# Anchoring row work behind pair work in the attention stripes of a four-layer graph network, and a new order of matmuls in its wide layer-2 pass

## The chip, the cores and the metric

The kernel runs on one core of a Trainium2 chip. The metric is the device time of one launch in microseconds (us). The kernel before was timed three times: 1152.08, 1147.19 and 1141.33 us, median 1147.19. One more execution was profiled: 1140.81 us, with a span of 1139.1 us from the first to the last instruction that the profile records, at a mean granted TensorE clock of 0.972. All single durations below come from that execution.

## The reference, cut to what matters

`x` has 4096 rows of 64 numbers; `adj` is a 4096 x 4096 matrix of zeros and ones. Four layers follow each other; each adds its result to its input and normalizes the rows. All four read the whole of `adj`.

```python
# layer 0: mean over neighbours, a linear layer, relu, rows to length 1
deg = clip(adj.sum(1) + 1, 1);  h = (adj @ X + X) / deg
out = relu(concat([X, h], 1) @ W + b);  out = out / max(norm(out), 1e-12)
# layers 1 and 3: attention in hyperbolic space
left, right = x_t @ w_att[:D], x_t @ w_att[D:]          # x_t = logmap0(x)
adj_att = sigmoid(left[:, None] + right[None, :] + b) * adj
x_local = logmap(x[:, None, :], x[None, :, :])          # a vector for each pair of rows
out = proj(expmap(x, einsum('ij,ijd->id', adj_att, x_local)))
# layer 2: halving weights by the rank of a neighbour, counted from the end of the row
support = x @ weight;  rank = cumsum(adj, 1)
k = min(deg, 100);  pos = rank - (deg - k)
out = (adj * where(pos > 0, 0.5 ** (k - pos), 0)) @ support + bias
# after every layer
x = layernorm(x + out)
```

## The kernel before, in words

**Tiling.** The 4096 target rows are four *groups* of 1024 (`GROUPS`, taken 3, 2, 1, 0), the 4096 source rows 32 *blocks* of 128 (`BLOCKS`, taken 31 to 0). A *stripe* is one group's pass over all source rows. Within a stripe the loop variable g runs from 15 to 0 and covers two blocks; `load(s, g)` on the SyncE queue (SP) brings their 1 MB of edges into one of six buffers, so all of `adj` (64 MB) is read once a layer. The text calls such a step of two blocks, inside a stripe, a *group of two blocks*, and numbers the eight attention stripes 0 to 3 (layer 1) and 4 to 7 (layer 3).

**Pair work in attention** (`attend`, L924 to L973). For each block six matmuls make z in PSUM for 128 x 1024 pairs (L945, L948, L951, two halves each); ScalarE (ACT) makes the sigmoid (L953) and a square of z (L956); VectorE (DVE) makes t1 (L959, per block) and, for both blocks at once, t2 (L961). PE then adds t2 into `acc` with four fp32 matmuls (L965, eight records in the trace). z, sig, sq and t have two buffers each. At the end of a stripe ACT copies `acc` to `sums` (L972).

**Row work.** What has to be done for a finished stripe's 1024 rows is written as Python generators. `later` puts one in one of two queues; after each block and each t2 `tick(rate)` runs the steps that are due, in both queues, until a step yields a wait (1 in the attention layers). rate is 1, but 2 in stripe 0 and 4 in stripe 4. Row PSUM buffers are two, taken by `take` after `free`. The generators that matter here:

- `move` (L982 to L1086) turns `sums` into the rows of the next layer's x: matmuls with `centre` (L1000), ACT's copy to u (L1002, twice), GpSimd's product w_att (L1007), the sums uu (L1011) and d (L1013) on DVE, then some 70 small DVE operations of 128 x 8 (k at L1015, three inverse square roots with the lines L673 to L679, tanh on ACT between, L1046 and on), at last GpSimd's w_att (L1081) and DVE's x (L1085).
- `linear` (L1088 to L1112) makes layer 2's products of those rows: transposes (L1095), ACT's copy x_t (L1100), matmuls (L1106), and `supports`, ACT's and DVE's `halves` (L1116, L1117).
- `spread_left` (L906 to L922) prepares the next group's left terms (L914 on PE); it is put in the second queue at g == 4 of the stripe before and is needed at the next stripe's start.
- `norm_rows` and `prepare` do the layer norm and the operands of the next attention layer.

After stripe n > 0 `attention` (L1280 to L1295) puts into the first queue `linear` (in layer 1) or `store` (in layer 3) of the group before, and then the move of the group just done. Only in the last stripe does `linear` go to the second queue, with a wait of 9.

**What sets the order.** In layers 0 and 2 a `manual_schedule` block keeps PE and ACT in the order of the source. In the attention layers (1 and 3) no such block holds: a scheduler places the instructions of every engine by what they depend on and by its own estimates, so a row step may end up ahead of pair work that stands before it in the source. Each engine then runs its list in order.

**Layer 2.** `wide_pass` (L1323 to L1351) takes groups 3 and 2 together: for each block and each of the two, `count` (L1386, four matmuls of 128 columns' weights) updates z, then the waiting `add_up` of the stripe-block before (L1401, four matmuls of 64-column weights) runs, then ACT makes the exponential (L1395). `narrow_pass` does groups 1 and 0 alone. `check` (L751) is a DVE operation over a loaded 128 x 2048 that sets a flag; every second load of layers 0 and 2 has one.

After layer 3 follow the last move, the last store and a few small checks: the *tail*. A second, general path of the kernel (behind a branch) isn't run here.

Of the kernel before, what the change touches and what calls it, by code (L numbers as in the profile page):

```python
# [19 lines left out]
P = 128  # L20
# [38 lines left out]
def gnn_stack_kernel(  # L59
# [509 lines left out]
    def stream(fits):  # L569

        with ExitStack() as st:
# [17 lines left out]
            FIXED = {mybir.EngineType.PE, mybir.EngineType.Activation}  # L589
            queues, place, done, held = ([], []), [0, 0], set(), []  # L590

            def tick(n):
                for _ in range(n):
                    place[1] += 1
                    for queue in queues:
                        while queue and queue[0][1] <= place[1]:
                            wait = next(queue[0][0], None)
                            if wait is None:
                                queue.pop(0)
                                continue  # L600
                            queue[0][1] = place[1] + wait
                            if wait:
                                break

# [3 lines left out]
            def in_turn(tag, *parts):  # L608
                for part in parts:
                    yield from (part or ())  # L610
                done.add(tag)

# [16 lines left out]
            def near():  # L629

                return 3 if place[0] == 0 else 1

# [36 lines left out]
            def rsqrt(a, name):  # L669
# [10 lines left out]
                return r  # L680

# [73 lines left out]
            def curved(c, name, least):  # L755


                c2, sc, rsc, of_y, root, short = (
                    num(keep, name + n, 1)
                    for n in ("_c2", "_sc", "_rsc", "_of_y", "_root", "_short")  # L760
# [3 lines left out]
                V.tensor_mul(root, rsc, c)  # L764
                V.tensor_scalar(of_y, rsc, -((2.0 * UNIT) ** -0.5), None, ALU.mult)
# [3 lines left out]
                return c, c2, sc, rsc, of_y, root, short  # L769
# [21 lines left out]
            def prepare(layer, s, att, b_att, curve, least, good, small):  # L791


                c, c2, sc, rsc, of_y, root, short = curve
# [187 lines left out]
            def move(layer, s, sums, curve):  # L982
# [3 lines left out]
                c, c2, sc, rsc, of_y, root, short = curve  # L986
# [22 lines left out]
                yield near()  # L1009
                yield soon()  # L1010
# [4 lines left out]
                V.scalar_tensor_tensor(k, d, c2, sum_1, ALU.mult, ALU.add)  # L1015
                V.tensor_mul(k, k, rb[:, at])

                kx, t2, xt = nums("kx"), nums("t2"), nums("xt")
                V.tensor_mul(kx, k, x2g)
                V.scalar_tensor_tensor(t2, d, -2.0, kx, ALU.mult, ALU.add)  # L1020
                V.tensor_mul(t2, t2, k)
                V.tensor_add(t2, t2, uu)
                V.tensor_scalar(t2, t2, 1e-30, None, ALU.max)
                V.tensor_sub(xt, d, kx)
                yield soon()
# [3 lines left out]
                V.scalar_tensor_tensor(un, t2, root, rsqrt(t2, "r_t2"), ALU.mult, ALU.mult)  # L1029
                V.tensor_scalar(un, un, fac, short, ALU.mult, ALU.max)  # L1030
                th = nums("th")
                V.reciprocal(r_un, un)
                yield after(29)
                nc.scalar.activation(th, un, AF.Tanh, scale=lam)
                yield near()
                V.scalar_tensor_tensor(un, r_un, fac, th, ALU.mult, ALU.mult)

                y2, xy, den, p, q = (nums(n) for n in ("y2", "xy", "den", "p", "q"))
                V.scalar_tensor_tensor(y2, un, c, un, ALU.mult, ALU.mult)
                V.scalar_tensor_tensor(xy, un, c2, xt, ALU.mult, ALU.mult)  # L1040
                V.tensor_mul(q, b[:, at], un)
                V.tensor_mul(y2, y2, t2)
                V.tensor_scalar(xy, xy, -1.0, 1.0, ALU.mult, ALU.add)
                V.tensor_mul(p, q, k)
                V.tensor_mul(den, cx2[:, at], y2)
                V.tensor_add(y2, xy, y2)  # L1046
                V.tensor_add(den, den, xy)
                V.tensor_sub(p, y2, p)
                V.tensor_scalar(den, den, 1e-15, None, ALU.max)
                V.reciprocal(den, den)  # L1050
                yield soon()
                V.tensor_mul(p, p, den)
                V.tensor_mul(q, q, den)

                px, qd, w2, t = nums("px"), nums("qd"), nums("w2"), nums("mt")
                V.tensor_mul(px, p, x2g)
                V.tensor_mul(qd, q, d)
                V.tensor_mul(t, q, q)
                V.scalar_tensor_tensor(w2, qd, 2.0, px, ALU.mult, ALU.add)
                V.tensor_mul(t, t, uu)  # L1060
                V.tensor_mul(w2, w2, p)
                V.tensor_add(px, px, qd)
                V.tensor_add(w2, w2, t)
                V.tensor_scalar(t, w2, least, None, ALU.max)
                yield soon()
                n = rsqrt(t, "n")
                V.tensor_scalar(n, n, rsc, 1.0, ALU.mult, ALU.min)
                yield soon()

                V.tensor_mul(w2, w2, n)  # L1070
                V.tensor_mul(p, p, n)
                V.tensor_mul(q, q, n)
                V.scalar_tensor_tensor(w2, px, 2.0, w2, ALU.mult, ALU.add)
                V.tensor_mul(w2, w2, n)
                V.tensor_add(w2, w2, x2g)
                V.tensor_scalar(w2, w2, 1.0 / D, 1e-5, ALU.mult, ALU.add)
                r = rsqrt(w2, "n")
                V.scalar_tensor_tensor(p, p, 1.0, r, ALU.add, ALU.mult)
                V.tensor_mul(q, q, r)  # L1079
                yield soon()  # L1080
                nc.gpsimd.tensor_mul(w, xg, over(p))  # L1081
                V.tensor_mul(u, u, over(q))
                yield soon()
                yield soon()
                V.tensor_add(x_of(layer + 1)[:, at, :], u, w)  # L1085
                yield after(72)  # L1086
# [193 lines left out]
            def attention(layer, curve, rates, behind):  # L1280

                need((layer, GROUPS[0]))
                for n, s in enumerate(GROUPS):
                    if n:
                        need((layer, s, "left"))
# [224 lines left out]
```

## Time and profile before

| What | us |
|---|---|
| Median of three runs | 1147.19 |
| Profiled execution | 1140.81 |
| Its span | 1139.1 |
| Layer 0 and stripe 0, to stripe 0's last t2 | 277.5 |
| Stripes 1, 2, 3 (from one last t2 to the next) | 81.2, 86.4, 87.2 |
| Layer 2's first exponential | at 529.2 |
| Layer 2's wide pass, two narrow passes | to 638.4, to 700.7, to 772.2 |
| Stripe 4's last t2 | at 863.9 |
| Stripes 5, 6, 7 | 81.2, 81.1, 83.4 |
| Tail, from stripe 7's last t2 to the end | 1109.6 to 1139.1 |

A row of the profile's timeline gives the start in us, the duration, engine, source line, operation, output and inputs with their shape, and in brackets how long the engine stood idle before it and which instruction released it. A row of the costliest groups gives the instructions' total busy time, the mean of one in ns, and the idle time ahead of them. A row of the waits gives which instruction waited for which, the total idle time, how often, and the longest.

### The profile page before, as it was taken

How to read it: one execution, taken by the hardware profiler on the slowest of the kernel's cores; microseconds unless marked ns; L12 is line 12 of the kernel's file. 1: busy time of each engine (PE TensorE's matmuls, PEld its weight loads, DVE VectorE, ACT ScalarE, POOL GpSimd, SP SyncE). 2: the span in 40 equal slices, each digit the busy share in tenths (PEclk: the TensorE clock that was granted, in tenths of full speed). 3: DMA queues.
4: the chain of work that ended last, by engine and by line, in shares of the span. 5: the costliest groups of instructions: out<-in, count | busy, mean ns of one | idle time of the engine just before them, and what ended most of it. 6: DMA issues, size and time to landing. Idle time of an engine off the chain costs nothing.

```text
span 1139.1 us, 13626 instructions
## 1 busy us (share of the span) xinstructions
PE 1021.6 (90%) x4949; PEld 391.2 (34%) x4949; DVE 956.0 (84%) x1882; ACT 821.2 (72%) x894; POOL 66.1 (6%) x97
## 2 busy tenths in 40 slices
PE   6999897899999899998999997798899999998981
PEld 3545544233333333332333232232333333333320
DVE  6687898999999899999653476528999999999996
ACT  0003216899989789787766778888898998987970
POOL 0020120000000000100100020000000001001001
PEclk8999998999999999999999999899999999999995
DMA  8999998545666466564988976676455665665500
GB/s 342 422 391 405 373 415 337 196 166 203 215 206 219 154 209 221 180 204 154 322 305 301 341 263 233 233 257 231 164 206 188 218 222 194 222 221 183 196 0 23
DMA packets 38419, 271.58 MB, mean 238 GB/s; under 512 B 4550, under 2 KB 4550, under 8 KB 5574
## 3 DMA queue, kind: packets, MB, share of 16 engines
q1 hardware_dynamic: 37440, 269.50, 65.8%
q10 hardware_dynamic: 902, 1.12, 0.3%
q8 instruction: 41, 0.67, 0.2%
q14 instruction: 36, 0.29, 0.1%
HBM read 269.55 MB, written 1.05 MB: 238 GB/s over the span
## 4 chain that ended last, share of the span: by engine, by line
DVE 53%; PE 29%; ACT 8%; DMA 6%; POOL 2%; issue 2%; ACTq 0%; SPq 0%; POOLq 0%; DVEq 0%
DVE t L959 21%; DVE t L961 20%; PE z L1386 10%; DMA edges<-in_adj_dram 6%; PE acc L1401 5%; PE acc L1243 4%; PE acc L965 2%; ACT sig L953 2%; ACT sq L956 2%; ACT sq L1395 1%; PE aux L1106 1%; PE aux L852 1%; PE z L945 1%; DVE junk L751 1%; PE z L951 1%
## 5 line engine op out<-in xcount | busy, mean ns | idle before, releaser
L953 ACT ACTIVATE sig<-left_b,right 128x1024 f32<-128x1024 f32 x256 | 293.8, 1149 | 46.5 <-DVE t L959 36.5
L959 DVE SCALAR_TENSOR_TENSOR t<-z,sig 128x1024 f32<-128x1024 f32 x256 | 310.0, 1216 | 5.9 <-ACT sq L956 5.0
L956 ACT ACTIVATE sq<-z,turn 128x1024 f32<-128x1024 f32 x256 | 281.5, 1106 | 22.8 <-PE z L951 20.7
L961 DVE SCALAR_TENSOR_TENSOR t<-sq,t 128x2048 f32<-128x2048 f32 x128 | 292.9, 2288 | 0.7
L965 PE MATMUL acc<-t,xe 128*64 128x512 f32 x1024 | 255.2, 611 | 28.5 <-DVE t L961 24.4
L945 PE MATMUL z<-edges,two_i 128*128 128x512 bf16 x512 | 201.7, 394 | 21.5 <-DVE t L959 21.5
L951 PE MATMUL z<-dst,src 74*128 74x512 f16 x512 | 195.2, 381 | 0.0
L948 PE MATMUL z<-lo_hi,hi_lo 128*128 128x512 f16 x512 | 194.1, 379 | 0.0
L1395 ACT ACTIVATE sq<-z,at_edge 128x512 bf16<-128x512 f32 (+1 forms) x192 | 153.0, 830 | 53.3 <-PE z L1386 51.9
L965 PEld LDWEIGHTS acc<-t,xe 128*64 128x64 f32 x1024 | 63.6, 137 | 163.0 <-DVE t L961 85.9
L751 DVE SCALAR_TENSOR_TENSOR t<-edges 128x2048 bf16<-128x2048 f32 x32 | 74.0, 2312 | 44.2 <-DMA edges<-in_adj_dram 44.1
L1386 PE MATMUL z<-edges,pass_by 128*128 128x512 bf16 x248 | 89.6, 401 | 15.9 <-ACT sq L1395 15.8
L945 PEld LDWEIGHTS <-two_i 128*128 128x128 bf16 x512 | 50.2, 98 | 143.8 <-issue 96.6
L1243 PE MATMUL acc<-edges,first 128*128 128x512 bf16 x256 | 80.6, 396 | 20.0 <-DMA edges<-in_adj_dram 19.8
L1386 PE MATMUL z<-edges,enter 128*128 128x512 bf16 x256 | 90.8, 397 | 0.0
L1401 PE MATMUL acc<-sq,halves 128*64 128x512 bf16 x512 | 82.6, 401 | 3.6 <-ACT sq L1395 2.9
L1243 PE MATMUL acc<-edges,third 128*65 128x512 bf16 x256 | 80.5, 396 | 0.0
L751 DVE SCALAR_TENSOR_TENSOR junk<-edges 128x2048 bf16<-128x2048 f32 x32 | 73.1, 2285 | 4.7 <-DMA edges<-in_adj_dram 4.5
L948 PEld LDWEIGHTS <-hi_lo 128*128 128x128 f16 x512 | 50.3, 98 | 68.8 <-issue 25.5
L951 PEld LDWEIGHTS <-src 74*128 74x128 f16 x512 | 49.2, 96 | 67.5 <-issue 2.3
L1081 POOL TENSOR_TENSOR w_att<-x,p 128x512 f32<-128x512 f32 x8 | 12.9, 1615 | 495.0 <-DVE q L1079 495.0
L1243 PEld LDWEIGHTS <-first 128*128 128x128 bf16 x256 | 24.1, 98 | 48.9 <-issue 21.3
(262 smaller groups left out, 771.3 us busy)
## 6 DMA issues: line engine op xcount, KB each, us to landing
edges<-in_adj_dram SPq DMA_DIRECT2D x256, 1024.0 KB, 4.9
x<-in_x_dram SPq DMA_DIRECT2D x4, 256.0 KB
out_dram<-x ACTq DMA_DIRECT2D x4, 256.0 KB
w_sb<-in_L_gnn_W_dram ACTq DMA_DIRECT2D x1, 32.0 KB, 5.1
given<-in_L_gnn_b_dram ACTq DMA_DIRECT2D x1, 0.2 KB
given<-in_L_gnn_bias_dram ACTq DMA_DIRECT2D x1, 0.2 KB
given<-in_L_gnn_b_att_dram ACTq DMA_DIRECT2D x1, 0.0 KB
given<-in_L_gnn_att_b_dram ACTq DMA_DIRECT2D x1, 0.0 KB
```

The source lines that it names most:

```text
L751: V.scalar_tensor_tensor(junk, a, 0.0, a, ALU.not_equal, ALU.not_equal, accum_out=odd[:, n : n + 1])
L945: nc.tensor.matmul(half, two_i, edge[:, at : at + W], start=True, stop=False)
L948: nc.tensor.matmul(half, hi_lo[:, of], lo_hi[:, to], start=False, stop=False)
L951: nc.tensor.matmul(half, src[:, of], dst[:, to], start=False, stop=True)
L953: nc.scalar.activation(sig, left_b, AF.Sigmoid, bias=right[:, j : j + 1])
L956: nc.scalar.activation(sq[:, k], zp, AF.Square, bias=turn, scale=-1.0 / UNIT)
L959: V.scalar_tensor_tensor(t[:, k], zp, 0.0, sig, ALU.max, ALU.mult)
L961: V.scalar_tensor_tensor(t, sq, HIGH**2, t, ALU.add, ALU.mult)
L965: nc.tensor.matmul(acc[h * D : (h + 1) * D, :], xe[:, j, :], t[:, k, h * W : (h + 1) * W], start=j == BLOCKS[0], stop=j == BLOCKS[-1],)
L1243: nc.tensor.matmul(accs[h][:m], lhs[:, j, :], edge[:, at : at + W], start=j == BLOCKS[0], stop=j == BLOCKS[-1],)
L1386: nc.tensor.matmul(z[:, h : h + W], lhs, rhs[:, h : h + W], start=j == BLOCKS[0], stop=True, skip_group_check=True,)
L1395: nc.scalar.activation(w, z[:, :n], AF.Exp, bias=at_edge, scale=-LN2)
```

## The change

- `mark` is called by `tick` ahead of the row steps and after them. It goes through the instructions written since its last call. Those on PE, ACT and DVE written outside the row steps are noted as the last pair instruction of their engine; each written by a row step gets a dependency without a semaphore, for the scheduler alone, on that last pair instruction. So in the scheduler's list it can't stand ahead of it. This holds in stripes with n > 0 (`anchored`), so not in stripes 0 and 4.
- `linear` and `store` of the group before go to the second queue in every stripe n > 0, with a wait of 9, and start only when the move of that group is through (`there`).
- In `wide_pass` both counts of a block come first, each with its exponential, and then both `add_up`s of the block before. Both accumulators are allocated at the start, and the two exponentials of a block share one buffer.
- In `move` the helper class `Small` is used with `on_pool` False, so all its operations stay on DVE. The reciprocal `r_un` of `un` is replaced by two operations on the inverse root (`by_root`, `by_short`, constants made once in `curved`), and one more yield stands behind d.

The instructions of PE, ACT, GpSimd and SP are the same in number; DVE gets 12 more small ones.

```diff
+            def mark(rows):
+                traced = nc.cur_bb.bb.instructions
+                for i in traced[seen[0] :]:
+                    if i.engine not in ROW_ENGINES:
+                        continue
+                    if not rows:
+                        pairs_last[i.engine] = i
+                    elif anchored[0] and i.engine in pairs_last:
+                        tc.add_manual_dep(
+                            i, pairs_last[i.engine].name,
+                            mybir.DependencyInfo(
+                                mybir.DependencyClass.NoSync, mybir.DependencyReason.DATA
+                            ),
+                            reason="row work behind the pairs",
+                        )
+                seen[0] = len(traced)
 
             def tick(n):
                 for _ in range(n):
                     place[1] += 1
+                    mark(False)
                     for queue in queues:
...
+                    mark(True)
...
+            def there(tag):
+                while tag not in done:
+                    yield 1
...
                 yield soon()
                 V.tensor_reduce(d, w, AX.X, ALU.add)
                 yield soon()
-                V.scalar_tensor_tensor(k, d, c2, sum_1, ALU.mult, ALU.add)
+                yield soon()
+                G.stt(k, d, c2, sum_1, ALU.mult, ALU.add)
...
-                V.reciprocal(r_un, un)
+                G.ts(r_un, r, by_root, 1.0 / fac, ALU.mult, ALU.mult)
+                G.ts(r_un, r_un, by_short, None, ALU.min)
...
+                    anchored[0] = n > 0
                     then = GROUPS[n + 1] if n + 1 < NW else None
                     sums = attend(layer, s, rates[n], then)
-                    move_s = move(layer, s, sums, curve)
+                    move_s = in_turn((layer, s, "moved"), move(layer, s, sums, curve))
                     if n:
-                        last = n + 1 == NW
-                        later(in_turn((layer + 1, s + 1), behind(s + 1)), last, 9 * last)
+                        later(
+                            in_turn((layer + 1, s + 1), there((layer, s + 1, "moved")), behind(s + 1)),
+                            True, 9,
+                        )
                     later(move_s)
                     if n + 1 == NW:
                         later(in_turn((layer + 1, s), behind(s)))
+                anchored[0] = False
...
-                accs = [None, None]
+                accs = [ps.tile([P, W], F32, name="acc") for _ in two]
...
+                        w = sb.tile([P, 2, WW], F32, name="sq").bitcast(BF16)[:, :, :WW]
                         for i, edge in enumerate(edges):
                             here = edge[:, k * WW : (k + 1) * WW]
                             count(zs[i], behind[i], here, j, WW)
                             behind[i] = here
-                            while lag:
-                                lag.pop(0)()
-                            w = weights_of(zs[i], WW)
-
-                            def add(i=i, j=j, w=w):
-                                if accs[i] is None:
-                                    accs[i] = ps.tile([P, W], F32, name="acc")
-                                add_up(accs[i], j, w[:, :W], w[:, W:])
-
-                            lag.append(add)
+                            weights_of(zs[i], WW, w[:, i])
+                            if i == 1:
+                                for of, acc in enumerate(accs if lag else ()):
+                                    add_up(acc, *lag[of])
+                                lag = [(j, w[:, n, :W], w[:, n, W:]) for n in range(2)]
```

## The prediction, made before the changed kernel ran

> **What bounds the kernel now.** I read the busy shares first, then the chain that ended last, then windows of each stage, then single groups of instructions.
>
> ```profile
> PE 1021.6 (90%) x4949; PEld 391.2 (34%) x4949; DVE 956.0 (84%) x1882; ACT 821.2 (72%) x894; POOL 66.1 (6%) x97
> DVE 53%; PE 29%; ACT 8%; DMA 6%; POOL 2%; issue 2%; ACTq 0%; SPq 0%; POOLq 0%; DVEq 0%
> 200.00:300.00 100.00, 91.27 (x429) 33.65 (x428) 95.74 (x134) 91.07 (x93) 3.47 (x8) 1.00 0.56 190
> 610.00:630.00 20.00, 20.00 (x105) 5.69 (x103) 4.83 (x6) 14.20 (x14) 0.00 (x0) 1.00 0.94 341
> ```
>
> The windows give sum, then PE, PEld, DVE, ACT and POOL busy, the granted clock, the DMA share and GB/s. In the attention stripes (200 to 300) PE, DVE and ACT are all nearly full; in the wide pass of layer 2 (610 to 630) PE never rests. An average can't tell which of three full engines sets a stripe, so I took one undisturbed group (two blocks) apart:
>
> ```profile
> 211.95 1.94 PE L965 MATMUL acc<-t,xe 128*64 128x512 f32 x8
> 213.02 0.15 DVE L679 SCALAR_TENSOR_TENSOR n_r<-rs_t,n_r 128x8 f32<-128x8 f32 x1
> 213.10 1.21 DVE L959 SCALAR_TENSOR_TENSOR t<-z,sig 128x1024 f32<-128x1024 f32 x1
> 213.82 0.40 PE L945 MATMUL z<-edges,two_i 128*128 128x512 bf16 x1
> 218.56 0.40 PE L945 MATMUL z<-edges,two_i 128*128 128x512 bf16 x1
> ```
>
> Groups start 4.74 us apart. PE's own work is 12 z matmuls at 0.2225 (2.67), 1.86 for the accumulation and about 0.2 for two changes between them: 4.73. DVE has t1 twice at 1.14 and t2 at 2.2, 4.47 in all, plus 0.085 for a small row operation slipped between (213.02 to the next start at 213.10). So three row operations in a group are free, and everything beyond is paid; every PE row matmul is paid at once (L1000 1.05 a call, layer 2's linear about 3.5 a group of rows). Both engines are the bound, group by group. DMA isn't: its share here is 0.56.
>
> **Anchoring the rows (`mark`) and the linear in the second queue.** Neither removes an instruction on PE or ACT, and DVE gains 12 (two scalings for one reciprocal in each of eight moves, and four constants): 8 x 0.085 = 0.7 spread over hidden places. What changes is where rows stand. Before, the scheduler put row steps early, where they waited in order:
>
> ```profile
> 383.44 0.69 DVE L1013 TENSOR_REDUCE d<-w_att 128x8 f32<-128x512 f32 x1 [3.48 <-POOL w_att L1007]
> 385.77 0.22 DVE L1015 SCALAR_TENSOR_TENSOR k<-d,k_c,u 128x8 f32<-128x8 f32 x1
> 388.33 2.35 DVE L959 SCALAR_TENSOR_TENSOR t<-z,sig 128x1024 f32<-128x1024 f32 x2
> 289.05 0.39 PE L945 MATMUL z<-edges,two_i 128*128 128x512 bf16 x1 [1.32 <-DVE t L959]
> ```
>
> DVE stood still 3.48 us for POOL's product, then ran 14 dependent operations in 2.6 us with nothing between, while t1 waited behind them and (in the analogous place, 289.05) PE waited for t1. In the changed order each row step stands behind the t1 or t2 ahead of it in the source, a few operations at a time.
>
> A rule speaks against a gain here: the Trainium skill, "VectorE: DVE Perf Modes", Rules for kernel authors, says of chained operations that the pipeline is flushed after each whatever one does, so only their number counts. By it this part is worth nothing (rival (a), 1144). The row says a dependent operation back to back costs 0.20, between pairs 0.085: twelve cost 2.4 or 1.0. I take the row.
>
> I summed for each stripe, over its 16 groups, the larger of 4.73 + PE rows and 4.47 + DVE rows, with the order of before and with the built order of the changed kernel. The stripes are numbered 0 to 7; 0 and 4 are not anchored and keep their PE order. Measured lengths are between the last t2 of one stripe and of the next.
>
> - Stripe 1: 79.9 by the sum, 81.2 measured; after 79.8.
> - Stripe 2: 85.7, 86.4; after 83.2 (layer 2's linear and the move no longer meet in one group, which had 8.7 and 7.2).
> - Stripe 3: 83.5, 84.9 without one layer-2 check; after 82.7.
> - Stripes 5, 6, 7: 79.9, 79.3, 80.5, measured 81.2, 81.1, 83.4; after 79.8, 81.0, 80.2.
>
> What measurement has over the sum is stalls and chains, some 0.4 to 2.9. After, I leave one: d is still read soon after ACT's copy of u and POOL's product. The nearest row is stripe 7's: POOL ends at 1045.51, DVE was free at 1044.42, 1.1 us late, of which DVE's three-operation slack and double buffers recover most. I take 0.3 in stripes 1 and 5 and 0.3 to 0.8 elsewhere; bounds are 0 and 3.5 (the 3.48 above). Queued behind d on DVE is the next t1, and PE's z, which has two buffers, waits for that. The linear now waits for its move to end; queued behind it are the columns for the next stripe (`spread_left`), which the built order still has in groups 11 and 12 of 16 at the latest, so nothing waits for them; SP's and POOL's instructions are the same in the same order. Stripe by stripe: -1.1, -2.9, -1.9, -1.1, +0.5, -2.4 (about 1 of which is a clock drop of this execution at 1038 to 1042), together -8.9.
>
> **Entry into layer 2.** Before, a check of 2.28 us stood ahead of the last t2, and PE waited for it; the new order has it behind.
>
> ```profile
> 527.74 2.28 DVE L751 SCALAR_TENSOR_TENSOR t<-edges 128x2048 bf16<-128x2048 f32 x1
> 532.36 1.94 PE L965 MATMUL acc<-t,xe 128*64 128x512 f32 x8 [0.33 <-DVE t L961]
> ```
>
> Not all 2.28 is gained: ACT's first exp, at 529.2 to 530.4, bounds PE next. I take -1.4 (0 to -2.3).
>
> **Both counts, then both adds.** The wide pass has the same matmuls in another order.
>
> ```profile
> 604.93 0.62 PE L1386 MATMUL z<-edges,pass_by 128*128 128x512 bf16 x2
> 605.94 0.62 PE L1401 MATMUL acc<-sq,halves 128*64 128x512 bf16 x4
> 606.10 1.11 ACT L1395 ACTIVATE sq<-z,at_edge 128x1024 bf16<-128x1024 f32 x1 [0.45 <-PE z L1386]
> 606.49 0.62 PE L1386 MATMUL z<-edges,pass_by 128*128 128x512 bf16 x2
> ```
>
> A stripe-block takes 1.56 (604.93 to 606.49). Counts start 0.2285 apart, but from a count to an add and back it is 0.315: a change between 128 and 64 columns costs some 0.09. Four per block become two: 3.12 to 2.95, times about 30 blocks = -5.2. The Trainium skill ("TensorEngine Tiling (Array Packing)", Key Properties) says that a change of tiling mode drains TensorE, without a figure: by that rule alone I couldn't size this, and the row bounds it. ACT needs 2 x 1.11 = 2.22 of the 2.95, and its adds come a block later, so it doesn't bound. The edges (2 MB a pair of blocks) would be asked at 355 GB/s for 336; the run shows 420 in layer 0 (20 to 60 us). If neither held, the gain is 0; I keep 0 to -5.6.
>
> **The tail.** One step of a move a pair makes it end later: x of stripe 2's move comes behind pair mark 17 for 8, stripe 3's 23 for 13. In stripe 7, with nothing behind, the remains of the move before fall behind the last t2, where nothing hides them.
>
> ```profile
> 1109.56 0.16 DVE L677 TENSOR_TENSOR rs_t<-n 128x8 f32<-128x8 f32 x1
> 1116.15 0.38 ACT L1002 COPY u<-aux 128x260 f32<-128x260 f32 x1 [2.50 <-DVE x L1085]
> 1124.57 0.17 DVE L1046 TENSOR_TENSOR y<-xy,y 128x8 f32<-128x8 f32 x1
> ```
>
> Before, they begin in the last root (L677), 6.5 us to x; the last move's u waits for them. After, they begin at L1046, 23 operations earlier: the last move shows L1046 to its next root (at 1126.58) taking 2.01, and seven operations of a root at 0.20 are 1.4. That is +3.4, all on the path (0 to +4). The two scalings for the reciprocal lie beside tanh: nothing there; uncovered, 0.2.
>
> **Sum.** -8.9 - 1.4 - 5.2 + 3.4 = -12.1 on the profiled execution (1140.81, span 1139.1). The median, 1147.19, is 6.4 above it; the clock drop is likely to recur somewhere, but it weighs 1, so I take the whole -12.1 from the median: 1135.1, told as 1135.
>
> **The rivals.**
> - (a) The attention keeps its time: PE's 4.73 and its row matmuls bind each group anyway, and a stall removed at one place returns at the next boundary. For it: the sums of stripes 1, 5 and 6 barely fall. Against: PE waits 21.5 us for t1 (below). Then 1147.2 - 6.6 + 3.4 = 1144.
> - (b) The wide pass gets no shorter, since edges come no faster than the 341 GB/s at a share of 0.94 above: 5.2 lost, 1140.
> - (c) More: the maxima per group smooth out through the buffers, down to PE's own sum (stripe 1: 75.7 + 2.1 = 77.8 for 79.8). At 1.5 in each of six stripes: 1126.
> - (d) Slower: DVE stands at d. In the anchored order it can't run a t1 ahead of d when u or POOL's product is late, so it may lose at every boundary what it lost at 383: 3.5, and 1.3 more until PE has filled z again (as at 289.05). Less the 0.5 taken, that is 4.3 in each of six stripes, 26 us: 1161. The gain is gone from 2.0 a stripe, and over 1% is lost from 3.9. For it: d's waits below, each of 1 to 3.5 us. Against: steps now lie at least one block (2.4 us) apart, and POOL's product takes 2.03.
>
> ```profile
> L945 PE MATMUL z<-edges,two_i 128*128 128x512 bf16 x512 | 201.7, 394 | 21.5 <-DVE t L959 21.5
> DVE d L1013 <- POOL w_att L1007: 7.3, 5, 3.5
> DVE halves L1117 <- ACT halves L1116: 10.7, 4, 5.1
> ```
>
> The first says that 21.5 us of PE's waiting are open to a gain; the others that d waits already, and `halves` too, but in layer 2.
>
> **How the numbers follow.** Forecast 0.50, (a) 0.15, (b) 0.11, (c) 0.16, (d) 0.08. The likeliest is 1135, its own range 1130 to 1140, from the bounds of the stall at d (-3 to +5 over six stripes) and of the entry and tail (1 each). The range 1126 to 1146 takes in (a) and (b), and leaves out (d) and the half of (c) beyond 1126. About 1% is what a measurement of this kernel can tell from none: below 1135.7 is faster, above 1158.7 slower. A little over half the forecast (0.28), nearly all of (c) (0.15) and a fifth of (a) and (b) (0.05) give 0.48 for faster; slower 0.05 out of (d); the rest, 0.47, within 1%.
>
> **What would show it.** In the wide pass blocks 2.95 apart, not 3.12. Stripes of 80 to 83.5. PE's wait at L945 for t1 falling from 21.5 to under 12; d's wait for POOL below 4. Last t2 to the end growing from 29.5 to 33. I am wrong if DVE loses over 2 us at each boundary, or if exp gaps open in the wide pass.

## The result and the profile after

The changed kernel took 1136.84 us, median of 20 runs (1132.65 to 1143.20); the kernel before, in 20 runs beside it, 1142.71 (1140.83 to 1152.08). The ratio is 0.9947, 95% interval 0.9929 to 0.9965: 0.5% faster, some 6 us. The forecast was 12 us below 1147.19, the median then known.

The profiled execution took 1134.03 us with a span of 1132.3. The busy shares of the engines (first row) are almost those of before, with PE and DVE both near full; so are the shares in the chain that ended last (second row):

```profile
PE 1014.7 (90%) x4949; PEld 396.4 (35%) x4949; DVE 955.3 (84%) x1894; ACT 818.9 (72%) x894; POOL 63.8 (6%) x97
DVE 50%; PE 31%; ACT 9%; DMA 5%; issue 2%; POOL 2%; ACTq 0%; SPq 0%; POOLq 0%; DVEq 0%
```

The groups of instructions show one wait smaller and another larger. t1 (L959 before, the first row) is L1036 here, the first z matmul (L945) is L1022:

```profile
L959 DVE SCALAR_TENSOR_TENSOR t<-z,sig 128x1024 f32<-128x1024 f32 x256 | 310.0, 1216 | 5.9 <-ACT sq L956 5.0
L1036 DVE SCALAR_TENSOR_TENSOR t<-z,sig 128x1024 f32<-128x1024 f32 x256 | 310.9, 1219 | 13.2 <-ACT sq L1033 11.9
L1022 PE MATMUL z<-edges,two_i 128*128 128x512 bf16 x512 | 201.2, 393 | 17.6 <-DVE t L1036 17.5
```

PE's wait for t1 fell from 21.5 to 17.5, not below 12; t1's own wait for ACT's square rose from 5.0 to 11.9.

Cutting both traces at the same events (the last t2 of each stripe, the exponentials of layer 2) gives the difference by stage. "Entry" runs from stripe 3's last t2 to the first exponential of layer 2, which comes before that t2's end, so it is negative.

| Stage | before | after | difference |
|---|---|---|---|
| layer 0 and stripe 0 | 277.6 | 278.8 | +1.2 |
| stripe 1 | 81.2 | 81.9 | +0.7 |
| stripe 2 | 86.4 | 83.5 | -2.9 |
| stripe 3 and entry | 84.1 | 82.0 | -2.1 |
| wide pass | 109.2 | 102.0 | -7.2 |
| first narrow pass | 62.3 | 63.6 | +1.3 |
| second narrow pass, stripe 4 | 163.2 | 160.5 | -2.7 |
| stripe 5 | 81.2 | 81.9 | +0.7 |
| stripe 6 | 81.1 | 82.1 | +1.0 |
| stripe 7 | 83.4 | 82.6 | -0.8 |
| tail | 29.4 | 33.3 | +3.9 |

In the anchored stripes each group repeats to within 0.2 us from trace to trace where the order is the same. What does not repeat is the clock. In every trace the granted clock stands at 0.50 in some stretches, before the tail of 3.4, 6.8 or 10.2 us each; I call that half clock. PE is slower there, and a stage that holds such a stretch can't be compared with one that doesn't.

The -2.7 comes from it: in the second narrow pass and stripe 4 the trace of before has 17.0 us at half clock and the trace of after 10.2. All nine traces with 17.0 take 163.1 to 163.5 there, all five with 10.2 take 160.4 to 160.8. The +1.2 is scatter: layer 0, which the change doesn't touch, ends anywhere from 179.0 to 183.7 in the fourteen traces. The wide pass of after holds 3.4 us of half clock (528.3 to 531.7): five other traces with the new pass and none there take 100.4 for its 102.0 (two more, which enter layer 2 in the order of before, 101.1). In stripe 7 both traces hold 3.4 us of it (from 1038.4 before, from 1064.2 after). The rest is what the change did: the wide pass gained, stripes 2 and 3 gained, stripes 1, 5, 6 and the tail lost.

**The wide pass** is now gapless with half the changes between counts and adds:

```profile
607.58 0.62 PE L1473 MATMUL z<-edges,pass_by 128*128 128x512 bf16 x2
608.04 0.61 PE L1473 MATMUL z<-edges,enter 128*128 128x512 bf16 x2
608.50 0.61 PE L1473 MATMUL z<-edges,pass_by 128*128 128x512 bf16 x2
608.75 2.12 ACT L1480 ACTIVATE sq<-z,at_edge 128x1024 bf16<-128x1024 f32 x2 [0.78 <-PE z L1473]
608.95 0.61 PE L1473 MATMUL z<-edges,enter 128*128 128x512 bf16 x2
609.49 1.05 PE L1485 MATMUL acc<-sq,halves 128*64 128x512 bf16 x8
610.48 0.62 PE L1473 MATMUL z<-edges,pass_by 128*128 128x512 bf16 x2
```

A block takes 2.90 (607.58 to 610.48) for 3.12: 0.22, a little over the 0.17 forecast. The edges kept up, at 346 GB/s and the same DMA share of 0.94 in a window of 20 us, in which PE never rests:

```profile
598.00:618.00 20.00, 20.00 (x112) 7.29 (x112) 9.45 (x9) 14.84 (x16) 0.00 (x0) 1.00 0.94 346
```

**Part of it came back in the narrow pass**, which the diff doesn't touch. In the order on DVE, a check (L824) now stands ahead of the chain that ends in y (L882); ACT's copy of y holds the exponentials behind it in its fixed order, and PE waits:

```profile
647.24 2.28 DVE L824 SCALAR_TENSOR_TENSOR t<-edges 128x2048 bf16<-128x2048 f32 x1
650.41 1.53 DVE L882 TENSOR_TENSOR y<-x,ym 128x512 f32<-128x512 f32 x1
651.98 0.62 ACT L885 CAST ys<-y 128x512 f16<-128x512 f32 x1 [3.07 <-DVE y L882]
654.27 0.39 PE L1473 MATMUL z<-edges,pass_by 128*128 128x512 bf16 x1 [4.15 <-ACT sq L1480]
```

Before, the same matmul waited 2.53 and the check (at 661.09) stood behind y (at 658.96). Between the two exponentials around this place lie 5.9 us in all eleven traces with the new wide pass, and 4.3 in the three with the old one: 1.6 us are given back.

### The profile page after: what moved, and what is told of

Same layout as the page of the kernel before. It is cut to its first block, busy times and chain, and to the rows that moved or that the text cites. A ratio compares the mean times of both kernels' runs of the same rounds, so it can differ in the third digit from the quotient of the medians.

```text
span 1132.3 us, 13600 instructions
## 1 busy us (share of the span) xinstructions
PE 1014.7 (90%) x4949; PEld 396.4 (35%) x4949; DVE 955.3 (84%) x1894; ACT 818.9 (72%) x894; POOL 63.8 (6%) x97
## 4 chain that ended last, share of the span: by engine, by line
DVE 50%; PE 31%; ACT 9%; DMA 5%; issue 2%; POOL 2%; ACTq 0%; SPq 0%; POOLq 0%; DVEq 0%
DVE t L1038 19%; DVE t L1036 18%; PE z L1473 9%; PE acc L1042 5%; PE acc L1485 5%; DMA edges<-in_adj_dram 5%; PE acc L1329 3%; ACT sq L1033 3%; PE z L1022 2%; DVE junk L824 2%; ACT sq L1480 2%; PE z L1028 2%; PE z L1025 2%; ACT sig L1030 2%; POOL sq L855 1%
## 5 line engine op out<-in xcount | busy, mean ns | idle before, releaser
L1036 DVE SCALAR_TENSOR_TENSOR t<-z,sig 128x1024 f32<-128x1024 f32 x256 | 310.9, 1219 | 13.2 <-ACT sq L1033 11.9
L1042 PE MATMUL acc<-t,xe 128*64 128x512 f32 x1024 | 256.7, 614 | 31.9 <-DVE t L1038 28.6
L1022 PE MATMUL z<-edges,two_i 128*128 128x512 bf16 x512 | 201.2, 393 | 17.6 <-DVE t L1036 17.5
L1028 PE MATMUL z<-dst,src 74*128 74x512 f16 x512 | 195.2, 381 | 0.0
L1480 ACT ACTIVATE sq<-z,at_edge 128x512 bf16<-128x512 f32 (+1 forms) x192 | 150.6, 829 | 45.0 <-PE z L1473 44.6
L1042 PEld LDWEIGHTS acc<-t,xe 128*64 128x64 f32 x1024 | 63.1, 137 | 165.6 <-DVE t L1038 82.7
L824 DVE SCALAR_TENSOR_TENSOR t<-edges 128x2048 bf16<-128x2048 f32 x32 | 73.0, 2287 | 41.1 <-DMA edges<-in_adj_dram 39.5
L1329 PE MATMUL acc<-edges,first 128*128 128x512 bf16 x256 | 81.6, 400 | 20.8 <-DMA edges<-in_adj_dram 20.6
L1022 PEld LDWEIGHTS <-two_i 128*128 128x128 bf16 x512 | 50.2, 98 | 137.8 <-issue 91.4
L1329 PE MATMUL acc<-edges,third 128*65 128x512 bf16 x256 | 81.8, 401 | 0.0
L824 DVE SCALAR_TENSOR_TENSOR junk<-edges 128x2048 bf16<-128x2048 f32 x32 | 73.1, 2286 | 7.1 <-DMA edges<-in_adj_dram 6.9
L1485 PE MATMUL acc<-sq,halves 128*64 128x512 bf16 x512 | 75.8, 395 | 0.2 <-ACT sq L1480 0.2
L1028 PEld LDWEIGHTS <-src 74*128 74x128 f16 x512 | 49.1, 96 | 66.8 <-issue 1.8
L1473 PEld LDWEIGHTS <-enter 128*128 128x128 bf16 x256 | 24.7, 98 | 48.1 <-issue 26.0
```

Of the source, the lines that this page charges most:

```text
L824: V.scalar_tensor_tensor(junk, a, 0.0, a, ALU.not_equal, ALU.not_equal, accum_out=odd[:, n : n + 1])
L1022: nc.tensor.matmul(half, two_i, edge[:, at : at + W], start=True, stop=False)
L1028: nc.tensor.matmul(half, src[:, of], dst[:, to], start=False, stop=True)
L1036: V.scalar_tensor_tensor(t[:, k], zp, 0.0, sig, ALU.max, ALU.mult)
L1042: nc.tensor.matmul(acc[h * D : (h + 1) * D, :], xe[:, j, :], t[:, k, h * W : (h + 1) * W], start=j == BLOCKS[0], stop=j == BLOCKS[-1],)
L1329: nc.tensor.matmul(accs[h][:m], lhs[:, j, :], edge[:, at : at + W], start=j == BLOCKS[0], stop=j == BLOCKS[-1],)
```

## Experiments: one part at a time

The first four runs ask which part brings what. `wide_only` takes the functions of the wide pass into the kernel before; `rows_only` is the changed kernel with the old ones. `no_anchor` and `faster_last` are one line each:

```diff
-                    anchored[0] = n > 0
+                    anchored[0] = False
```
```diff
-            attention(3, curve3, (4, 1, 1, 1), store)
+            attention(3, curve3, (4, 1, 1, 2), store)
```

> The kernel before with only the new order of counts and adds in layer 2's wide pass. Theory (the parts add up, and the wide pass brings more than the row work): blocks 2.90 apart, 7 us off the wide pass, ratio 0.994, with the attention stripes (81.2, 86.4, 87.2) and the tail (29.5 us) as before. Rival (the anchored row work brings most): under 3 us, ratio 0.998 or more.

> The changed kernel with the old wide pass. Theory: what stripes 2, 3 and the entry into layer 2 gain (some 6 us) is paid back in stripes 1, 5, 6 (2.4) and in the tail (3.8), ratio 0.998 to 1.002. Rival (the row work brings most): ratio 0.995 or less.

> The changed kernel with no row step tied to the pairs; the second queue, the wide pass and the two scalings stay. Theory (the anchor makes the moves end later and the tail longer, and doesn't shorten stripes 1 and 5): stripes 1 and 5 at 81.2, tail back at 29 to 31, stripe 2 at 83 to 84 by the second queue alone; 1133 to 1137. Rival (the anchor is what brings stripes 2 and 3 down): stripes 2 and 3 at 86 again, 1140 or more.

> The changed kernel with two row steps a pair instead of one in the last stripe of layer 3. Theory (the move of the stripe before that is left over at the end lies open in the tail): the tail falls from 33 by about 10, the last stripe grows by 1 to 4 since more than three row operations stand in some groups; 1129 to 1134. Rival (the tail is set by the last move alone): the tail stays at 33, 1137 to 1140.

Measured, with the ratio to the kernel before and stages from the traces. The kernel before was timed beside each set of runs, on the same chip (median 1144.01 for these four, 1143.05 and 1143.73 for the two sets below), so ratios are to be compared, not medians. `faster_last` has six runs, the others eleven or more.

| Run | median us | ratio (interval) | s1 | s2 | s3 + entry | wide | s5 | s6 | s7 | tail |
|---|---|---|---|---|---|---|---|---|---|---|
| before | | 1 | 81.2 | 86.4 | 84.1 | 109.2 | 81.2 | 81.1 | 83.4 | 29.4 |
| after | 1136.84 | 0.9947 (0.9929 to 0.9965) | 81.9 | 83.5 | 82.0 | 102.0 | 81.9 | 82.1 | 82.6 | 33.3 |
| wide_only | 1140.53 | 0.9962 (0.9942 to 0.9982) | 81.2 | 86.4 | 85.7 | 101.1 | 81.2 | 81.1 | 83.5 | 29.5 |
| rows_only | 1142.18 | 0.9989 (0.9977 to 1.0002) | 81.9 | 83.5 | 82.0 | 108.0 | 81.9 | 82.1 | 82.6 | 33.0 |
| no_anchor | 1138.54 | 0.9957 (0.9944 to 0.9969) | 81.5 | 85.2 | 84.3 | 100.4 | 81.5 | 83.1 | 83.0 | 29.5 |
| faster_last | 1136.19 | 0.9934 (0.9911 to 0.9956) | 81.9 | 83.5 | 82.0 | 100.4 | 81.9 | 82.1 | 82.8 | 30.5 |

The parts add up within their intervals: 0.38% from the wide pass, 0.11% (not told from nothing) from all the row work, against 0.53% together. In the wide pass 8 us went and 1.6 came back in the narrow one. The row work gains in stripes 2 and 3 about what it pays in 1, 5, 6 and the tail. (Stripe 3 of `wide_only` holds a drop of the clock to half from 488.4 to 491.8, some 1.6 us.) Without the anchor the tail is the old 29.5, as expected; stripe 2 lies between before and after, so what stays in `no_anchor` (the second queue above all) brings some of its gain and the anchor the rest. Stripe 3 with the entry reads 84.3, the old 84, but its trace has half clock from 460.6 to 464.0, where z matmuls start 0.42 apart for 0.22. I estimate from these rows that some 1.6 us of it are the clock's, so this run doesn't show what the anchor brings to stripe 3. The time, 1138.5, lies between the two theories.

`faster_last` missed: the tail fell by 2.8, not 10. At twice the rate 29 operations of the move before are still left behind the last t2, for 49 at rate 1. The rate only says when a step may be written. The likely reason, which no run tested: the scheduler lays a chain of dependent operations one or a few to a slot between DVE's pair operations, and a stripe has 48 such slots.

## Experiments: what keeps stripes 1 and 5 long

In stripes 1 and 5 DVE stood idle 2.9 us in one group, waiting for ACT's square. I first put it down to the second `centre` call, which stands inside a z block there; the rival was GpSimd's product:

```diff
-                    yield near()
+                    yield near() + (place[0] != 0 and part == 0)
```
```diff
-                nc.gpsimd.tensor_mul(w, xg, u)
+                V.tensor_mul(w, xg, u)
```

These are `u_gap` and `dve_u`. Two more ask which tie moves what: `anchor_dve` ties DVE's row operations alone, `anchor_12` ties all three engines in the last two stripes of layer 1 alone:

```diff
-                    if i.engine not in ROW_ENGINES:
+                    if i.engine != mybir.EngineType.DVE:
```
```diff
-                    anchored[0] = n > 0
+                    anchored[0] = n in (2, 3) and layer == 1
```

> The changed kernel with one more wait between the two centre calls of a move, which in the built order puts the second call right behind the first (blocks 2.83 and 3.0 of the stripe) where it had stood at 3.83, behind the accumulation and ahead of the last z matmul of its block. Theory (that place makes z of this block late, and t1 with it by 2.5): stripes 1 and 5 fall from 81.9 to 80 or less. In stripes 2, 6 and 7 up to 15 row operations now stand in one slot, so these grow by 1 to 2; 25 operations are left over at the end for 49, tail 29.5. Rival (GpSimd's product makes t1 late): stripes 1 and 5 stay at 81.9.

> The changed kernel with the product of x and u on VectorE in place of GpSimd, all else in the same order. Theory (GpSimd and VectorE hold each other up only where t2 or u's product meets GpSimd, 1.1 in stripe 6 and 0.95 of 1.8 in stripe 7; stripes 1 and 5 lose their time at z): stripes 1 and 5 grow by 0 to 0.6, stripe 6 81.5, stripe 7 82.3. Rival (waiting for GpSimd's product at the boundary is what the forecast missed): stripes 1 and 5 fall by 2, stripes 2, 3 and 6 by 1.

> The changed kernel with VectorE's row operations alone tied to the pairs, TensorE's and ScalarE's not. Theory (the tie on TensorE and ScalarE is what moves the centre calls and makes the moves end later): tail 29.5, stripes 1 and 5 at 80.5 or less, stripes 2, 6, 7 longer by 1 to 2 through 14 operations in one slot. Rival (the tie on VectorE is what counts): all stripes and the tail as in the changed kernel.

> The changed kernel with row steps tied only in the last two stripes of layer 1, where the runs showed a gain. Theory (stages add up): stripes 1 and 5 81.5, 2 and 3 83.5 and 83.1, 6 and 7 83, tail 29.5; 3 us less than the changed kernel, 1132 to 1135. Rival (time moved out of the tail comes back in the last stripes): 1136 to 1138.

| Run | median us | ratio (interval) | s1 | s2 | s3 + entry | s5 | s6 | s7 | tail |
|---|---|---|---|---|---|---|---|---|---|
| u_gap | 1142.11 | 0.9999 (0.9984 to 1.0013) | 81.7 | 87.8 | 83.7 | 81.7 | 82.7 | 82.3 | 29.4 |
| dve_u | 1136.13 | 0.9946 (0.9921 to 0.9970) | 82.4 | 83.9 | 82.4 | 82.3 | 81.6 | 81.0 | 32.5 |
| anchor_dve | 1138.87 (one run) | not timed in rounds | 81.3 | 85.4 | 82.9 | 81.3 | 82.9 | 83.4 | 29.4 |
| anchor_12 | 1135.56 | 0.9949 (0.9932 to 0.9966) | 81.5 | 84.2 | 81.7 | 81.5 | 83.1 | 82.8 | 29.4 |

`dve_u` and `anchor_12` have six runs each. Stripes 6 and 7 of `anchor_12` and `anchor_dve` hold 3.4 us of half clock each, and so does stripe 2 of `anchor_dve`.

Both explanations of stripes 1 and 5 fell. With the second call moved (`u_gap`) stripe 1 still took 81.7, with 2.8 us of DVE idle; with the product on DVE (`dve_u`) 82.4, with 2.9. What `dve_u` did show is a smaller cause in stripes 6 and 7: 0.5 less in stripe 6, as expected, and 1.6 less in stripe 7, where 0.3 was expected. (Not all of the 1.6 need be GpSimd's: stripe 7 holds half clock in the changed kernel and none in `dve_u`.) GpSimd and DVE hold each other up, in the trace of the changed kernel:

```profile
962.37 2.29 DVE L1038 SCALAR_TENSOR_TENSOR t<-sq,t 128x2048 f32<-128x2048 f32 x1
963.66 2.04 POOL L1084 TENSOR_TENSOR w_att<-x,u 128x512 f32<-128x512 f32 x1 [3.56 <-ACT u L1079]
965.73 0.69 DVE L1090 TENSOR_REDUCE d<-w_att 128x8 f32<-128x512 f32 x1 [1.08 <-POOL w_att L1084]
...
1059.83 1.18 POOL L1084 TENSOR_TENSOR w_att<-x,u 128x512 f32<-128x512 f32 x1 [3.48 <-DVE t L1036]
1059.91 3.24 DVE L1038 SCALAR_TENSOR_TENSOR t<-sq,t 128x2048 f32<-128x2048 f32 x1
```

At 963.66 the product starts inside t2 and takes 2.04 for 1.18, so d waits 1.08; at 1059.83 it starts 0.08 ahead of t2, and t2 takes 3.24 for 2.29. Beside t1, which reads z from PSUM, both keep their time: in the run `acc_late`, told below, the product takes 1.19 beside two t1 of 2.55 together.

```profile
285.76 2.55 DVE L1062 SCALAR_TENSOR_TENSOR t<-z,sig 128x1024 f32<-128x1024 f32 x2 [0.64 <-ACT sq L1059]
286.08 1.19 POOL L1104 TENSOR_TENSOR w_att<-x,u 128x512 f32<-128x512 f32 x1 [56.34 <-ACT u L1099]
```

The Trainium skill ("SBUF — State Buffer", Who interferes with whom) says just this: a VectorE instruction with two SBUF inputs and a GpSimd instruction that reads SBUF exclude each other, the later one blocks. Weighed in the prediction, it would have put d's 1.08 into stripe 6 whole and 0.95 for t2 into stripe 7.

`anchor_dve` and `anchor_12` hit on the tail and missed by up to 0.8 us in stripes 1, 2 and 5. With the tie on DVE alone, or none in layer 3, the tail keeps its 29.4: the 3.9 us belong to tying PE and ACT there. `anchor_12` did no better than the changed kernel by its ratio, though 3 us less were expected. In its trace the six stripes, the entry and the tail do take 3.1 less together, but layer 0 and stripe 0 take 4.1 more; why the medians show no gain stays open.

Then the order of PE gave it away. In an undisturbed group the accumulation of one group (L965 before, L1042 after) stands behind all twelve z matmuls of the next. Counting where it stands otherwise, in the built orders:

| Kernel | accumulations that stand behind fewer than 12 z matmuls (stripe: how many) |
|---|---|
| before | 1: 9; 2: 6; 3: 11; 5: 9; 6: 10; 7: 10 |
| after | 1: 11; 5: 11 |
| u_gap | 1: 9; 2: 10, 10; 3: 10; 5: 9; 6: 10; 7: 10 |

(The last of layer 1 and of layer 3 aside.) After, stripe 1 looks so:

```profile
283.41 0.38 PE L1025 MATMUL z<-lo_hi,hi_lo 128*128 128x512 f16 x1
283.73 1.94 PE L1042 MATMUL acc<-t,xe 128*64 128x512 f32 x8
284.05 1.23 DVE L1036 SCALAR_TENSOR_TENSOR t<-z,sig 128x1024 f32<-128x1024 f32 x1 [0.37 <-ACT sq L1033]
285.60 0.71 PE L1077 MATMUL aux<-centre,sums 128*128 128x130 f32 x4
286.15 0.38 PE L1028 MATMUL z<-dst,src 74*128 74x512 f16 x1
286.62 1.12 ACT L1033 ACTIVATE sq<-z,turn 128x1024 f32<-128x1024 f32 x1
287.77 1.22 DVE L1036 SCALAR_TENSOR_TENSOR t<-z,sig 128x1024 f32<-128x1024 f32 x1 [2.50 <-ACT sq L1033]
```

Eleven z matmuls are issued by 283.6. The accumulation comes next, as t2 ends, and takes 1.9; the row matmuls follow, and the twelfth z matmul (L1028) starts at 286.15. So z of this block is done 2.5 us late, ACT's square with it, and DVE stands idle for 2.50 ahead of t1.

The test ties each accumulation behind the twelve, by writing it after the z matmuls of the next group and giving it a dependency for the scheduler alone on the last of them (`add_owed` issues the four matmuls of the oldest group owed, each with this dependency):

```diff
                             nc.tensor.matmul(half, src[:, of], dst[:, to], start=False, stop=True)
+                        if owed and k == 0:
+                            add_owed()
...
-                    for k in (1, 0):
...
+                    owed.append((g, t))
                     tick(rate)
+                add_owed()
                 sums = row.tile([P, W], F32, name="sums", bufs=2)
```

`late_dve_u` adds the product on DVE (six runs), `late_no_anchor` takes the rows' tie out (four runs), `before_late` is the kernel before with this edit alone.

> The changed kernel with each accumulation tied behind the twelve z matmuls of the next group. In the order of the changed kernel one accumulation at the start of stripes 1 and 5 stands after eleven of the twelve, everywhere else after all. Theory (that accumulation, waiting for t2, keeps z of the next block back, and t1 with it): the 2.9 us of VectorE's idle time there go, stripes 1 and 5 fall from 81.9 to 79.8 by the sum of the prediction, the others stay within 0.5, tail 1.4 less (42 operations left over for 49); 1131. Rival (the centre calls and ScalarE's copies of u make t1 late, wherever the accumulation stands): stripes 1 and 5 stay at 81.5 or more; 1136.

> The same with the product of x and u on VectorE. Theory (the two causes are apart, so their gains add up): on top of acc_late stripe 6 0.5 less and stripe 7 1.6 less, stripes 1 to 3 and 5 0.2 to 0.5 more, tail 1 more; 1130 to 1131. Rival (the later accumulation already frees VectorE from waiting for GpSimd): 0.6 more in each stripe, 1134.

> As acc_late, with no row step tied to the pairs. Theory (what the tie of the rows brought was the place of the accumulation): stripes within 1 us of acc_late's, tail 1 less. Rival (the tie of the rows has a worth of its own): stripes 2 and 3 longer by 1.5 to 2 each, as they were in the run without it.

> The kernel before with the accumulations tied in this way and nothing else. Theory: stripes 1 and 5 79.8 for 81.2, stripe 7 81 for 83.4, with the centre calls of stripes 2 and 3 far back (blocks 13.5 and 22) since layer 2's products still stand ahead of the move; tail 33 for 29.4 (47 operations left over for 26); ratio 0.994 to 0.998. Rival: stripes as before, ratio 1.00 to 1.003.

| Run | median us | ratio (interval) | s1 | s2 | s3 + entry | s5 | s6 | s7 | tail |
|---|---|---|---|---|---|---|---|---|---|
| acc_late | 1130.55 | 0.9899 (0.9870 to 0.9927) | 79.8 | 83.2 | 82.7 | 79.8 | 82.1 | 81.8 | 32.0 |
| late_dve_u | 1134.29 | 0.9918 (0.9887 to 0.9949) | 80.2 | 83.8 | 83.2 | 80.2 | 81.8 | 82.4 | 32.3 |
| late_no_anchor | 1129.32 | 0.9872 (0.9836 to 0.9908) | 80.1 | 82.7 | 82.3 | 80.1 | 81.7 | 82.6 | 31.6 |
| before_late | 1137.53 | 0.9945 (0.9933 to 0.9958) | 79.5 | 84.5 | 81.7 | 79.5 | 81.4 | 81.3 | 32.8 |

Stripes 1 and 5 fell to 79.8, the sum of the prediction. The same place in `acc_late` (its z matmuls are L1046 to L1052, t1 L1062, the accumulation L1017, `centre` L1097):

```profile
283.30 1.05 PE L1097 MATMUL aux<-centre,sums 128*128 128x130 f32 x8
284.86 0.38 PE L1052 MATMUL z<-dst,src 74*128 74x512 f16 x1
285.30 0.38 PE L1049 MATMUL z<-lo_hi,hi_lo 128*128 128x512 f16 x1
285.52 0.38 PE L1052 MATMUL z<-dst,src 74*128 74x512 f16 x1
285.83 1.94 PE L1017 MATMUL acc<-t,xe 128*64 128x512 f32 x8
```

Two blocks of z are through before the accumulation starts, two t1 run back to back (285.76, shown above), and 0.64 of waiting is left. The group at this place is 2.1 us shorter (7.65 to 5.51), which is what stripe 1 gains as a whole. The second `centre` call moved too, in front of the z block (283.30, both calls); no run moved the accumulation alone. But `u_gap` has the second call in front and the accumulation still early, and DVE waits as before:

```profile
282.23 0.61 PE L1077 MATMUL aux<-centre,sums 128*128 128x130 f32 x4
283.44 1.94 PE L1042 MATMUL acc<-t,xe 128*64 128x512 f32 x8
287.32 2.55 DVE L1036 SCALAR_TENSOR_TENSOR t<-z,sig 128x1024 f32<-128x1024 f32 x2 [2.35 <-ACT sq L1033]
```

So moving the call isn't enough, and what `acc_late` has beside it is the place of the accumulation.

`before_late` is the sharpest of these runs: one tie on the accumulation, and no anchor, takes 9.4 us off stripes 1 to 3 and 5 to 7 and the entry together (497.4 to 488.0), where the whole row work of the change takes 3.4 (to 494.0). (Some 1 us of the 9.4, by the prediction's estimate, is a clock drop in stripe 7 of before that `before_late` lacks.) It pays 3.4 of it again in the tail. With the accumulation tied, the rows' anchor brings nothing more: 489.6 with it, 489.5 without; and since `before_late` is at 488.0, neither does the rest of the change's row work. The tie with the new wide pass alone was not run. `late_no_anchor` is the fastest kernel run, 1.3% below before; it isn't told from `acc_late`.

The gain of `dve_u` didn't add to that of `acc_late`. The time is the rival's 1134, though the intervals overlap; of its 0.6 more in each stripe, stripes 1, 2, 3 and 5 show 0.3 to 0.6, stripe 6 shows 0.4 less. Stripe 7, 82.4 where 80.2 was expected, tells little: its trace has half clock from 1064.5 to 1067.9, and one group takes 6.31 that took 4.76 in `dve_u`.

## Why the prediction was half right

The direction held, and the time lay within the range, 1136.84 for 1135. That was in part luck. The 12.1 us were taken off 1147.19, the median of three runs; twenty runs put the kernel before at 1142.71. So the base was 4.5 too high and the gain, 5.9 measured, 6.2 too large, and the two errors nearly cancel. Of the signs named, the blocks of the wide pass (2.90), the stripes (81.9 to 83.5) and the tail (33.3) came; PE's wait for t1 fell to 17.5 and not under 12, d's wait for GpSimd from 7.3 to 4.8 and not below 4. By the prediction's own steps:

- **Wide pass, forecast -5.2, at most -5.6.** Right in mechanism, too small: -7.2 in this trace in spite of the half clock, and -7.6 between two traces without it that have the same entry (108.0 in `rows_only`, 100.4 in `faster_last`). A block gained 0.22 for 0.17. Count matmuls start 0.228 apart, adds in pairs some 0.225 apart; 8 counts and 4 pairs make 2.72, so two changes cost 0.18 of the 2.90. Before, 4 counts and 2 pairs, 1.36, left 0.20 of 1.56 for two changes, so four cost 0.40: 0.22 a block over some 30 blocks is 6.6 of the 7.6. Not forecast were the 1.6 us given back in the narrow pass, since I took DVE's order in layer 2 as unchanged where PE's was.
- **Stripes, forecast -8.9, measured -3.1** (+0.7 - 2.9 - 1.8 + 0.7 + 1.0 - 0.8, stripe 3 against 84.9 without the check). This is the step that failed, in the sentence "After, I leave one [stall]: d", at 0.3 to 0.8. In stripes 2 and 3 that was true: 83.5 and 83.1 for sums of 83.2 and 82.7. In stripes 1 and 5 the stall that stayed wasn't d's but z's, 2.9 us, behind an accumulation one matmul too early. The trace of before had it too:

```profile
282.48 1.94 PE L965 MATMUL acc<-t,xe 128*64 128x512 f32 x8
286.41 2.10 ACT L956 ACTIVATE sq<-z,turn 128x1024 f32<-128x1024 f32 x2
287.69 0.17 DVE L678 SCALAR_TENSOR_TENSOR rs_t<-rs_t,t 128x8 f32<-128x8 f32 x1
287.78 2.35 DVE L959 SCALAR_TENSOR_TENSOR t<-z,sig 128x1024 f32<-128x1024 f32 x2
```

The accumulation stands behind nine z matmuls, and the first of the two squares that t1 follows ends at 287.50. DVE's chain of eleven small operations (from 285.83, L678 the last) ends at 287.86. So the chain that I counted as the cost lay over the late z: without it t1 could have started some 0.3 earlier, no more. The place of the accumulation stood in the built order that I used for the sums, but I looked at how many row matmuls were in a group, not at where the pair matmuls stood. In stripe 6 d's 1.08 counted whole, in stripe 7 GpSimd took 0.95 from t2 and 0.85 from u's product (1.53 for 0.68).

- **The Trainium skill's rule on chained operations (named in the prediction).** That only their number counts fits stripe 1 of the changed kernel (chain spread out, no gain); the row's 0.085 fits `acc_late` (79.8, its sum), where most of the stall that hid it is gone. No run varied the placing of the small operations alone.
- **Entry, forecast -1.4.** Right, though part of it shows only later. Stripe 3 and the entry, to the first exponential, lost 2.1 where 3.3 was forecast. The other 1.2 lie behind that exponential: in `rows_only`, which has the old wide pass, that pass takes 108.0 for 109.2. The half clock of this trace lies behind it too. Counts of layer 2 stand ahead of the last accumulation, PE waits 1.77 for their exponential, and then the accumulation takes 3.41; in `faster_last`, with the same wait and the clock at 1.00, it takes 1.94:

```profile
527.42 0.61 PE L1473 MATMUL z<-edges,pass_by 128*128 128x512 bf16 x2 [1.77 <-ACT sq L1480]
527.96 3.41 PE L1042 MATMUL acc<-t,xe 128*64 128x512 f32 x8
528.40:531.60 3.20, 3.20 (x9) 0.62 (x6) 1.57 (x4) 0.19 (x1) 0.00 (x0) 0.50 0.00 0
```

The third row is a window: after the busy times comes the granted clock, 0.50.

- **Tail, forecast +3.4.** Measured +3.9, by the mechanism named: the remains of the move before begin at its y (L1046 before, L1128 here), and the last u waits for the x of that move.

```profile
1098.90 0.16 DVE L1128 TENSOR_TENSOR y<-xy,y 128x8 f32<-128x8 f32 x1
1108.91 0.38 ACT L1079 COPY u<-aux 128x260 f32<-128x260 f32 x1 [5.56 <-DVE x L1171]
```

- **The rivals.** (a) was nearest in kind, a stall that is taken away at one place and stands at another, though at the same boundary and only in some of the stripes. (b) fell: the edges came as fast as asked. (c) fell: no stripe went below its sum. (d) fell: d never lost over 1.1 us.

So of the 12.1 us forecast 5.8 were missing in the stripes, and the tail took 0.5 more. The wide pass brought 2.4 more than forecast; in this trace 1.6 of that went to the half clock and 1.3 back in the narrow pass.

## What to carry to other kernels

When a sum of engine times per group falls short of the measured stripe, look on each engine for a pair instruction that stands out of its usual turn, before putting the gap down to the wait that the trace names: in stripes 1 and 5 an accumulation one matmul too early, not the chain of small operations beside it, was the cost. A stall under another stall shows nothing until the first is gone, so price a removed chain only by what else is late at that moment. If the order is a scheduler's, tie the one instruction whose place matters rather than everything around it. And before a stage of one trace is compared with that of another, look at the granted clock in both: here a stretch of half clock moved a stage by as much as the parts of the change did.

## What the runs showed of the hardware that I had not expected

GpSimd's 128 x 512 product and DVE operations with two SBUF inputs ran one after the other: t2 3.24 for 2.29, u's product 1.53 for 0.68, GpSimd's own products 2.04 for 1.18 (L1084) and 3.04 for 1.04 (L1167), but no change beside t1. The adds with 64 columns of weights start two by two, 3 ns apart, and the pairs some 0.225 us apart, while counts with 128 columns start singly at 0.228. The granted clock was 1.00 or 0.50 and nothing between in all fourteen traces. At 0.50 z matmuls start 0.42 us apart for 0.22, and 3.4 us of it cost up to some 1.6 us (the wide pass of the changed kernel, stripe 3 of `wide_only`). What brings such a stretch about stays open.
